# A two-layer graph and attention network on one core: softmax row sums folded by DMA, and three smaller edits

## The chip, the core and the metric

The kernel runs on one core of a Trainium2 chip. The core has a matrix engine (TensorE, PE in the profile), a vector engine (VectorE, DVE), a scalar engine (ScalarE, ACT), a general engine (GpSimd, POOL) and a queue engine that issues transfers (SyncE, SP). Each works through its own instructions in order[...]. The metric is device time in microseconds (us) of the whole program, lower is better. Everything is in 32-bit floats.

## The reference

The input x is 16 batches of 1024 nodes with 256 channels; adj is a 1024 x 1024 matrix. Cut to what matters:

```python
# layer 0
A_hat = A_norm * dinv[:, None] * dinv[None, :]
agg = jnp.einsum('nm,bmd->bnd', A_hat, features)
h = jax.nn.relu(_batchnorm(agg.reshape(-1, d) @ W1.T + b1, g1, be1))
out = _batchnorm(h @ W2.T + b2, g2, be2)
x = _layernorm(x + out)
# layer 1
c_adj = mean of x over channels                      # one number per node
Wg = adj * 2 * | |sigmoid(c_m - c_n) - 0.5| - 0.5 |  # gates, per batch
q = relu(einsum('bcn,bnm->bcm', x^T, Wg) * para)     # queries, 4 heads of 64
k, v = split(x @ kv_w)
attn = softmax(q k^T * scale)
x = _layernorm(x + attn @ v)
```

The batch norms need statistics over all batches, so layer 0 runs in two phases before layer 1 can begin.

## The kernel before

**Layer 0.** The first phase (to about 607 us) multiplies the normalised adjacency with x and then with W1 for every batch, and keeps statistics; products of 2 x 2 blocks are formed with seven multiplications (`seven`, L104). Results go to DRAM in units of half a batch (four chunks of 128 x 512), except the last four units, those of batches 14 and 15, which stay in SBUF. The second phase (L454 to L547, to about 800 us) normalises each chunk with a ReLU on ScalarE (`first`, L476), combines chunks on DVE and POOL (L488, L509 to L513), multiplies by W2 and by sums of blocks of W2 (`SV`, L463 to L467), and stores the result. It starts with the two batches that stayed, whose 16 chunks L525 to L528 normalise before anything else on ScalarE.

**Layer 1: `fast` (L571).** Batches follow one another. One batch of attention is 16 steps: two halves of 512 queries, times two pairs of heads, times four steps over the keys. A step is `scores` (q and k on PE into PSUM, L787), `exps` (ScalarE, L799, one step ahead), `sums` (DVE adds the exponentials into an accumulator `acc` of 128 partitions x 2 heads x 512 queries, L805 and L808) and `attend` (PE multiplies with v, L823). At the fourth step ScalarE and DVE form the output `ot` (L834, L835), which goes to DRAM (`put_o`). Four steps make a block; a batch has four blocks, one for each pair in each half. "Third block" below means first pair of the second half.

Between the blocks stand the pieces of other work: the next batch's gates (`wg_a` on ScalarE, `wg_b` on DVE), its keys and values (L736, L747, from `x1T`), its queries (`graph`, L761), and for the batch after that the loading (`load`), scaling (`bn2_q`, POOL, L614), transposing (`rows`, DVE, L618), layer norm (`ln1_a` with statistics on DVE and POOL, `ln1_b` on ScalarE, L646), and the way of the result through DRAM back into `x1T` (`put_x1`, `get_x1`, and `x1_v` on DVE, L669). `crow` (L683) broadcasts the channel means through DRAM; the gates read it.

**Row sums.** `acc` holds, for each query, 128 partial sums on 128 partitions. `dens` (L846) adds them up with four matmuls by a column of ones (L852), ScalarE copies the result (L854), and four small transfers put it beside `ot` in DRAM, in rows 256 and up of `o_dram` (`DR` = 8 rows for each head). `fetch_o` (L881) loads output and sums back with eight transfers for a half, `finish_a` (L891) transposes both in one DVE instruction (L900), takes reciprocals (L903), scales (L905), adds the residual (L910) and takes the statistics of the layer norm; `finish_b` (L919) applies it on ScalarE and stores. The last half of the last batch (`by_pe`, L812) skips DRAM: `back` (L874) transposes on PE, `recips` (L863) the sums.

**The order.** A table gives each piece a slot; a slot is two steps, a block is two slots. `put` (L961) enters a piece, `arrange` (L1052) orders the pieces of a slot by `rank` (L1033), and the loop at L1178 issues all pieces of a block's two slots, then its four steps. `between` holds pieces that are issued behind a given step instead. `sums` of a block's first step is issued behind the last "short" PE piece of the block (`behind`, L1181; `dens` is one), or at the very front when there is none. Each engine's queue follows this order.

```python
            for k in range(len(now) + 1):
                if k == behind and 0 <= g < nsteps:
                    sums(g)
                if k < len(now):
                    f, a = now[k]
                    f(*a)
```

Pools concerned: `accp` (2 accumulators, L405), `ob` (2 fetched tiles), `ps_t` (4 PSUM tiles for all but the scores), `ps_s` (2 PSUM tiles for the scores), `ep` (6 exponential tiles, three steps).

Of the kernel before, what the change touches and what calls it, by code (L numbers as in the profile page):

```python
# [9 lines left out]
F32 = mybir.dt.float32  # L10
AF = mybir.ActivationFunctionType
OP = mybir.AluOpType
AX = mybir.AxisListType
# [3 lines left out]
P = 128  # L17
EPS = 1e-5
HEADS = 4
# [3 lines left out]
def gnn_norm_attention_kernel(  # L23
# [57 lines left out]
    Q = 32  # L81
# [1 line left out]
    y_blk = [yT_all[b].rearrange("i (d e) (q n) -> q e (i d) n", e=Q, q=NQ) for b in range(B)]  # L83


    DR = 8
    CD = C + HEADS * DR
    o_dram = {(b, h): dram.tile([NT // NH, CD, P], F32, name=f"o{b}_{h}") for b in range(B) for h in range(NH)}
    x1_dram = {
# [39 lines left out]
    with ExitStack() as l0:  # L129
        w0 = l0.enter_context(tc.tile_pool(name="w0", bufs=1))  # L130
        hp = l0.enter_context(tc.tile_pool(name="hp", bufs=9))
        W1T = w0.tile([P, CT, H], F32, name="W1T")
        W2T = w0.tile([P, HT, C], F32, name="W2T")
# [4 lines left out]
        hT = {}  # L138
# [10 lines left out]
        def bn_affine(mv, rs, c, g, be, bias, s, t, name):  # L149
# [6 lines left out]
            nc.vector.tensor_mul(s[:, col], rs, g[:, col])  # L156
            nc.vector.scalar_tensor_tensor(t[:, col], mu, s[:, col], be[:, col], op0=OP.mult, op1=OP.add)

        s1 = w0.tile([P, HT], F32, name="s1")
        t1 = w0.tile([P, HT], F32, name="t1")  # L160

        with ExitStack() as ph1:
# [220 lines left out]
            for b in range(B):  # L383
                other = hidden_blocks(b - 1) if b > 0 else iter(())
                for k, _ in enumerate(aggregate(b)):
                    next(other, None)
                    if b > 0 and k == 3:
                        sums_x(b + 1)
                for _ in other:
                    pass  # L390
            for f in range(HT):
                for h in range(NH):
                    u = (B - 1) * NH + h
                    if f == 0:
                        hT[u] = hp.tile([P, HT, FB], F32, tag="h", name=f"hT{u}")
                    p = hidden(B - 1, h, f)
                    nc.scalar.copy(hT[u][:, f, :], p)
                    nc.vector.bn_stats(st1[:, f, u, :], p)
                bn_affine(*bn_moments(st1, f, "bn1"), f, g1t, be1t, b1t, s1, t1, "bn1")
# [2 lines left out]
        right = lambda name, bufs: ctx.enter_context(tc.tile_pool(name=name, bufs=bufs, side="right"))  # L402
        keep = right("keep", 1)
        ldp = right("ldp", LDP)
        accp = right("accp", 2)  # L405
        RD = keep.tile([P, B * NT + 1, HEADS], F32, name="RD")
        ones32 = keep.tile([P, 32], F32, name="ones32")
        stq = keep.tile([P, 2, C // Q], F32, name="stq")
# [45 lines left out]
        with ExitStack() as ph2:  # L454
# [3 lines left out]

            KF = HT // 2
            wq = [[W2T[:, j * KF : (j + 1) * KF, ts(i, P)] for j in range(2)] for i in range(CT)]
            SV = tmp.tile([P, 4, KF, P], F32, tag="SV", bufs=1, name="SV")  # L463
            nc.gpsimd.tensor_add(SV[:, 0], wq[1][0], wq[1][1])
            nc.gpsimd.tensor_sub(SV[:, 1], SV[:, 0], wq[0][0])
            nc.gpsimd.tensor_sub(SV[:, 2], wq[0][0], wq[1][0])
            nc.gpsimd.tensor_sub(SV[:, 3], wq[0][1], SV[:, 1])  # L467
            ws = {1: wq[0][0], 2: wq[0][1], 3: SV[:, 3], 4: wq[1][1], 5: SV[:, 0], 6: SV[:, 1], 7: SV[:, 2]}
            KB_ = KEEP // NH
            pairs = [list(range(B - KB_, B))] + [[b, b + 1] for b in range(0, B - KB_, 2)]  # L470
# [5 lines left out]
            def first(u, fs=range(HT)):  # L476
                for f in fs:
                    nc.scalar.activation(
                        hT[u][:, f, :], hT[u][:, f, :], AF.Relu, bias=t1[:, f : f + 1], scale=s1[:, f : f + 1]
                    )  # L480
# [41 lines left out]
                                hT.pop(u_)  # L522
                    yield

            for fs in (range(KF), range(KF, HT)):  # L525
                for h in range(NH):
                    for b in pairs[0]:
                        first(b * NH + h, fs)  # L528
            for k, pair in enumerate(pairs):
                ahead = [b * NH + h for b in pairs[k + 1] for h in range(NH)] if k + 1 < len(pairs) else []  # L530
                for u in ahead:
# [21 lines left out]
    NP = HEADS // 2  # L553
# [17 lines left out]
    def fast():  # L571
      with ExitStack() as fx:
# [202 lines left out]
        def step(g):  # L775
            b, s = divmod(g, NS)
            hf, pair, cp = s // (NP * NT // 2), s // (NT // 2) % NP, s % (NT // 2)
            return b, hf, pair, cp
# [17 lines left out]
        def exps(g):  # L796
            for a in range(2):
                E[g, a] = ep.tile([P, 2, FB], F32, tag="e", name=f"e{g}_{a}")
                nc.scalar.activation(E[g, a], S.pop((g, a)), AF.Exp)  # L799

        def sums(g):
            b, hf, pair, cp = step(g)
            if cp == 0:
                ACC[b, hf, pair] = accp.tile([P, 2, FB], F32, tag="acc", name=f"acc{g}")
                nc.vector.tensor_add(ACC[b, hf, pair], E[g, 0], E[g, 1])  # L805
            else:
                for a in range(2):
                    nc.vector.tensor_add(ACC[b, hf, pair], ACC[b, hf, pair], E[g, a])  # L808
# [2 lines left out]

        def by_pe(b, hf):  # L812
            return b == B - 1 and hf == NH - 1

        def attend(g):
            b, hf, pair, cp = step(g)
# [24 lines left out]
        def put_o(b, hf, rows_, t):  # L841
            nc.sync.dma_start(
                o_dram[b, hf][:, rows_, :].rearrange("i p n -> p i n"), t.rearrange("p (i n) -> p i n", n=P)
            )

        def dens(b, hf):  # L846
            p = ps_t.tile([P, FB], F32, tag="t", name="pd")
            for pair in range(NP):
                acc = ACC.pop((b, hf, pair))
                for h in range(2):  # L850
                    k = 32 * (2 * pair + h)
                    nc.tensor.matmul(p[k : k + 32, :], ones32, acc[:, h, :], start=True, stop=True)  # L852
            DT[b, hf] = otp.tile([P, FB], F32, tag="dt", bufs=1, name=f"dt{b}_{hf}")
            nc.scalar.copy(DT[b, hf], p)  # L854
            if not by_pe(b, hf):
                for k in range(HEADS):
                    put_o(b, hf, slice(C + k * DR, C + (k + 1) * DR), DT[b, hf][32 * k : 32 * k + DR, :])

# [32 lines left out]
        def finish_a(b, j):  # L891
            hf, k = divmod(2 * j, KB)
            pool_r = (rp, "r") if b < B - 1 or not by_pe(b, hf) else (x1p, "x1")
            rd = RD[:, b * NT + 2 * j : b * NT + 2 * j + 2, :]
            if by_pe(b, hf):
                r = pool_r[0].tile([P, 2, C], F32, tag=pool_r[1], name=f"r_{b}_{j}")
                p = OB.pop((b, j))
            else:
                t = pool_r[0].tile([P, 2, CD], F32, tag=pool_r[1], name=f"r_{b}_{j}")
                nc.vector.transpose(  # L900
                    t.rearrange("p a c -> p (a c)"), OB.pop((b, j)).rearrange("p a c -> p (a c)")
                )
                nc.vector.reciprocal(rd, t[:, :, C:].rearrange("p a (h r) -> p a h r", r=DR)[:, :, :, 0])  # L903
                p = r = t[:, :, :C]
            nc.vector.tensor_mul(  # L905
                r.rearrange("p a (h d) -> p a h d", h=HEADS),
                p.rearrange("p a (h d) -> p a h d", h=HEADS),
                rd.unsqueeze(3).to_broadcast([P, 2, HEADS, HD]),
            )
            nc.vector.tensor_add(r, r, x1s.pop((b, j)))  # L910
            mv, rs = ln_stats(sm, r, f"z{b}_{j}")
            nm = sm.tile([P, 2], F32, tag="nm", name=f"nm_{b}_{j}")
            for a in range(2):
                nc.gpsimd.tensor_scalar(
                    nm[:, a : a + 1], mv[:, a, 0:1], rs[:, a : a + 1], -1.0, op0=OP.mult, op1=OP.mult
                )
            R[b, j] = (r, rs, nm)
# [43 lines left out]
        def put(w, t, f, *a):  # L961
            at.setdefault(w * NC + t, []).append((f, a))
# [4 lines left out]
        for b in range(B):  # L967

            for hf in range(NH):
                t = (hf + 1) * (NC // NH)  # L970
                put(b, t, dens, b, hf)
                if by_pe(b, hf):
                    put(b, t, recips, b, hf)
                for k in range(KB // 2):
                    j = hf * (KB // 2) + k

                    if b * NH + hf < B * NH - 3:
                        t_f, t_a, t_b = (t + 1, t + 2 + k, t + 6 + k) if hf == 0 else (t + 1, t + 4 + k, t + 6 + k)
                    elif not by_pe(b, hf):

                        t_f, t_a, t_b = t, t + 2 * k, t + 2 + 2 * k if b < B - 1 else (t + 2, NC + 1)[k]
                        if b == B - 1 and k == 0:
                            between[(b * NC + t_b) * 2 + NK // 2] = [(finish_b, (b, j))]
                            t_b = None
                    else:
                        t_f, t_a, t_b = t, t + 1 + k, t + 2 + k
                    put(b, t_f, back if by_pe(b, hf) else fetch_o, b, j)
                    if t_a == t:
                        between[(b * NC + t) * 2 + NK // 2] = [(finish_a, (b, j))]
                    else:  # L990
                        put(b, t_a, finish_a, b, j)
                    if t_b is not None:
                        put(b, t_b, finish_b, b, j)
# [36 lines left out]
        nsteps = B * NS  # L1030


        order = (dens, recips, x1_t, finish_a, fetch_o, finish_b, x1_v, rows, ln1_a, ln1_b, put_x1, get_x1, means, load, crow)  # L1033
        rank = {f: k for k, f in enumerate(order)}
        short = (dens, recips, x1_t, back)

# [327 lines left out]
```

## Time and profile before

| | us |
|---|---|
| median of 10 runs (2459.5 to 2462.69) | 2460.13 |
| the profiled execution: its own time | 2459.8 |
| its span, first to last instruction | 2458.1 |
| attention stage, about | 880 to 2430 |

| group | count | mean ns |
|---|---|---|
| L808 DVE add into acc | 384 | 1325 |
| L799 ACT exponential | 512 | 1020 |
| L852 PE row-sum matmul instructions | 256 | 612 |
| L854 ACT copy of the row sums | 32 | 588 |
| L900 DVE transpose in `finish_a` | 62 | 768 |
| L669 DVE transpose into x1T | 56 | 699 |
| L478 ACT normalisation of a chunk of layer 0, kept units | 16 | 801 |

In a timeline line the first number is the start in us from the span's beginning, the second the time that the merged run of instructions took, then engine, source line, operation, output<-input, shapes and how often; a bracket gives the idle time before it and what ended it. Matmuls of several column groups overlap, so the busy time of a group (the first number behind the bar in a group's row) says more than its mean. A table of windows gives, for a stretch, the busy time of PE, PE's weight loads, DVE, ACT and POOL, then PE's granted clock, the share of the 16 DMA engines and GB/s. The program issues each 32-bit matmul as two PE instructions.

### The profile page before, as it was taken

The numbers are of one execution on the slowest core, as the hardware profiler recorded it, in microseconds if no ns is written. First come the engines' busy times: TensorE is split into PE (matmuls) and PEld (weight loads), VectorE is DVE, ScalarE is ACT, GpSimd is POOL, SyncE is SP. The second block draws the span as 40 slices with busy tenths as digits, with TensorE's granted clock in tenths as the row PEclk, the third lists the DMA queues.
The fourth block names the chain that finished last, engine by engine and source line by source line (L and its number), as shares of the span: only waits on it lengthen the run. The fifth ranks groups of instructions, "written<-read, shape, count | busy, mean of one in ns | idle before, by whom it ended". The sixth has DMA issues, their size and how long they took to land. (4 is left out here: it accounts for less than half of the span.)

```text
span 2458.1 us, 33873 instructions
## 1 busy us (share of the span) xinstructions
PE 2409.4 (98%) x12217; PEld 1007.1 (41%) x12217; DVE 1810.9 (74%) x2583; ACT 1093.9 (45%) x1549; POOL 776.0 (32%) x826
## 2 busy tenths in 40 slices
PE   8999999999999899999999999999999999999997
PEld 4444444444444443443434434344344343443432
DVE  5545545556776777888788888888888878888676
ACT  2000000002554455564655656656566465564644
POOL 2222232221556531414224133232342322414012
PEclk9999999999999999999999999999999999999998
DMA  3122122222578544544544535545364454554221
GB/s 137 69 86 103 69 86 103 88 83 86 202 271 275 133 121 87 139 126 111 144 106 124 147 87 150 119 120 149 82 149 110 121 146 97 138 129 108 68 43 51
DMA packets 583951, 292.73 MB, mean 119 GB/s; under 512 B 407528, under 2 KB 556512, under 8 KB 576608
## 3 DMA queue, kind: packets, MB, share of 16 engines
q1 hardware_dynamic: 583776, 290.49, 43.2%
q8 instruction: 98, 1.61, 0.3%
q14 instruction: 77, 0.63, 0.1%
HBM read 194.46 MB, written 95.94 MB: 118 GB/s over the span
## 5 line engine op out<-in xcount | busy, mean ns | idle before, releaser
L799 ACT ACTIVATE e<-s 128x1024 f32<-128x1024 f32 x512 | 495.8, 1020 | 327.7 <-PE s L787 264.7
L808 DVE TENSOR_TENSOR acc<-acc,e 128x1024 f32<-128x1024 f32 x384 | 508.7, 1325 | 112.8 <-ACT e L799 86.5
L787 PE MATMUL s<-qT,kT 64*64 64x512 f32 x4096 | 490.6, 594 | 4.4 <-ACT e L799 1.7
L823 PE MATMUL o<-e,v 64*64 64x512 f32 x4096 | 485.3, 589 | 0.0
L761 PE MATMUL pg<-wg,x 128*128 128x512 f32 x960 | 426.5, 597 | 0.0
L614 POOL TENSOR_TENSOR yt<-yt,stq 128x512 f32<-128x512 f32 x120 | 183.8, 1532 | 412.9 <-DMA yt<-yT 236.0
L761 PEld LDWEIGHTS pg<-wg,x 128*128 128x128 f32 x960 | 178.7, 190 | 238.6 <-issue 237.8
L823 PEld LDWEIGHTS o<-e,v 64*64 64x64 f32 x4096 | 156.6, 133 | 282.8 <-issue 275.1
L787 PEld LDWEIGHTS s<-qT,kT 64*64 64x64 f32 x4096 | 147.2, 133 | 298.4 <-issue 254.1
L107 ACT COPY u<-pa 128x512 f32<-128x512 f32 x15 | 8.8, 585 | 475.3 <-PE pa L312 475.3
L66 POOL TENSOR_SCALAR rs_z<-mv_z 128x2 f32<-128x2 f32 x64 | 18.2, 285 | 470.6 <-DVE mv_z L563 449.7
L720 DVE SCALAR_TENSOR_TENSOR wg<-wg,adj 128x1024 f32<-128x1024 f32 x128 | 163.5, 1308 | 2.8
L312 PE MATMUL pa<-AhT,x 128*128 128x512 f32 x360 | 161.8, 592 | 0.0
L646 ACT ACTIVATE x<-x,nm_a,rs_a 128x256 f32<-128x256 f32 x128 | 75.8, 594 | 171.6 <-POOL nm_a L636 171.2
L835 DVE TENSOR_TENSOR ot<-o,ot 128x512 f32<-128x512 f32 x64 | 44.3, 691 | 130.9 <-ACT ot L834 130.9
L747 PE MATMUL pv<-kvw,x1T 128*128 128x256 f32 x512 | 118.2, 384 | 0.0
L736 PE MATMUL pk<-x1T,kvw 128*128 128x512 f32 x256 | 117.9, 604 | 0.0
L343 PE MATMUL ph<-agg,SW 128*128 128x512 f32 x240 | 112.8, 592 | 0.0
L66 POOL TENSOR_SCALAR rs_a<-mv_a 128x2 f32<-128x2 f32 x64 | 38.0, 593 | 234.6 <-DVE mv_a L563 233.4
L747 PEld LDWEIGHTS pv<-kvw,x1T 128*128 128x128 f32 x512 | 96.8, 192 | 31.7 <-issue 16.2
L312 PE MATMUL pa<-T,sx 128*128 128x512 f32 x240 | 107.9, 592 | 0.0
L312 PEld LDWEIGHTS pa<-AhT,x 128*128 128x128 f32 x360 | 68.4, 190 | 86.1 <-issue 86.1
(193 smaller groups left out, 3142.3 us busy)
## 6 DMA issues: line engine op xcount, KB each, us to landing
adj<-in_adj_dram SPq DMA_DIRECT2D x128, 512.0 KB
h<-hT SPq DMA_DIRECT2D x28, 1024.0 KB
hL<-h SPq DMA_DIRECT2D x28, 1024.0 KB
ob<-o SPq DMA_DIRECT2D x248, 72.0 KB
x<-in_x_dram SPq DMA_DIRECT2D x16, 1024.0 KB
yT<-y SPq DMA_DIRECT2D x64, 256.0 KB
out_dram<-r SPq DMA_DIRECT2D x64, 256.0 KB
xr<-in_x_dram SPq DMA_DIRECT2D x62, 256.0 KB
```

The costliest lines, as they stand in the source:

```text
L312: nc.tensor.matmul(p, xs[n][:, k, :], bs[n][:, k, :], start=(k == 0), stop=(k == KN - 1))
L343: nc.tensor.matmul(p, ws[n][:, ts(f, P)], bs[n], start=True, stop=True)
L614: nc.gpsimd.tensor_tensor(y, y, sc, op)
L646: nc.scalar.activation(r, r, AF.Identity, bias=nm[:, a : a + 1], scale=rs[:, a : a + 1], accum_out=css[b][:, i : i + 1])
L720: nc.vector.scalar_tensor_tensor(t, t, 1.0, adjs[b * NT + i], op0=OP.add, op1=OP.mult)
L736: nc.tensor.matmul(p, kvw[:, k, ts(c, P)], x1Ts[b][:, k, ts(h, FB)], start=(k == 0), stop=(k == CT - 1))
L747: nc.tensor.matmul(p[:, ts(a, C)], x1Ts[b][:, k, ts(j + a, P)], kvw[:, k, C:], start=(k == 0), stop=(k == CT - 1),)
L761: nc.tensor.matmul(pg[b], x1s[b, k // 2][:, k % 2, ts(c, P)], wgs[b, k][:, ts(h, FB)], start=(k == 0), stop=(k == NT - 1))
L787: nc.tensor.matmul(t[r * HD : (r + 1) * HD, h, :], kTs[b, pair][h * HD : (h + 1) * HD, ts(2 * cb + r, HD)], qTs[b, pair, hf][h * HD : (h + ...
L799: nc.scalar.activation(E[g, a], S.pop((g, a)), AF.Exp)
L808: nc.vector.tensor_add(ACC[b, hf, pair], ACC[b, hf, pair], E[g, a])
L823: nc.tensor.matmul(O[b, hf, pair][r][h * HD : (h + 1) * HD, :], vs[b][r * HD : (r + 1) * HD, cb, pair * P + h * HD : pair * P + (h + 1) * HD],
```

## The change

Three things change in layer 1 and one in layer 0.

1. **Row sums through DMA.** For all but the last three halves (`by_dma`), `dens` is gone. Instead POOL issues two accumulating transfers for each pair (`fold`): partitions 64 to 127 of `acc` are added onto 0 to 63, then, behind the block's second step, 32 to 63 onto 0 to 31. A block later `put_den` writes the remaining 32 rows for each head to DRAM. So `DR` is 32 instead of 8, `fetch_o` loads 384 rows instead of 288 and comes two slots later, and `finish_a` transposes sums and output in two instructions and adds the 32 rows with a `tensor_reduce`. `accp` has three buffers. For the first half of a batch `finish_a` moves from the start of the fourth block to behind the block's second and fourth steps.
2. **Last step of the program.** Its exponentials aren't added into `acc` on DVE; the row-sum matmuls of the last pair take them as further operands.
3. **Last pair of output tiles** is scaled with eight ScalarE instructions instead of one on DVE.
4. **Second phase's first chunks.** The first unit of each of the two batches comes first on ScalarE; of the next unit two chunks are normalised on DVE (two instructions each); the block sums of W2 (`SV`) are formed before the first phase's end instead of behind it.

```diff
-    DR = 8
+    DR = Q
...
+            SV = w0.tile([P, 4, KF, P], F32, name="SV")
+            wq = [[W2T[:, j * KF : (j + 1) * KF, ts(i, P)] for j in range(2)] for i in range(CT)]
+            nc.gpsimd.tensor_add(SV[:, 0], wq[1][0], wq[1][1])
...
-        accp = right("accp", 2)
+        accp = right("accp", 3)
...
-            for fs in (range(KF), range(KF, HT)):
-                for h in range(NH):
-                    for b in pairs[0]:
-                        first(b * NH + h, fs)
+            for fs in (range(KF), (KF,), (KF + 1,)):
+                for b in pairs[0]:
+                    first(b * NH, fs)
+            u = pairs[0][0] * NH + 1
+            for f in range(KF, HT):
+                t = hT[u][:, f, :]
+                nc.vector.tensor_scalar(t, t, s1[:, f : f + 1], t1[:, f : f + 1], op0=OP.mult, op1=OP.add)
+                nc.vector.tensor_scalar(t, t, 0.0, None, op0=OP.max)
+            first(u, range(KF))
+            for b in pairs[0][1:]:
+                first(b * NH + 1)
...
         def sums(g):
             b, hf, pair, cp = step(g)
+            if g == nsteps - 1:
+
+                EX[b, hf, pair] = [E[g, a] for a in range(2)]
+                return
...
+        def by_dma(b, hf):
+            return b * NH + hf < B * NH - 3
+
+        def fold(b, hf, pair, n):
+            acc = ACC[b, hf, pair]
+            nc.gpsimd.dma_start(acc[:n], acc[n : 2 * n], accum_op=OP.add)
+
+        def put_den(b, hf, pair):
+            acc = ACC.pop((b, hf, pair))
+            for h in range(2):
+                r = C + (2 * pair + h) * DR
+                put_o(b, hf, slice(r, r + DR), acc[:DR, h, :])
...
-                    nc.tensor.matmul(p[k : k + 32, :], ones32, acc[:, h, :], start=True, stop=True)
+                    more = EX.get((b, hf, pair), [])
+                    for n, t in enumerate(more + [acc]):
+                        nc.tensor.matmul(
+                            p[k : k + 32, :], ones32, t[:, h, :], start=n == 0, stop=n == len(more)
+                        )
...
+                p = r = pool_r[0].tile([P, 2, C], F32, tag=pool_r[1], name=f"r_{b}_{j}")
+                den = otp.tile([P, 2, CD - C], F32, tag="den", bufs=1, name=f"den_{b}_{j}")
+                ob = OB.pop((b, j))
+                nc.vector.transpose(den, ob[:, :, C:])
+                nc.vector.transpose(r, ob[:, :, :C])
+                den = den.rearrange("p a (h r) -> p a h r", r=DR)
+                if by_dma(b, hf):
+                    nc.vector.tensor_reduce(rd, den, AX.X, OP.add)
+                    nc.vector.reciprocal(rd, rd)
+                else:
+                    nc.vector.reciprocal(rd, den[:, :, :, 0])
+            if j == NT // 2 - 1 and by_pe(b, hf):
+
+                for a in range(2):
+                    for h in range(HEADS):
+                        nc.scalar.mul(r[:, a, ts(h, HD)], p[:, a, ts(h, HD)], rd[:, a, h : h + 1])
...
-                put(b, t, dens, b, hf)
+                if by_dma(b, hf):
+                    for pair in range(NP):
+
+                        s = b * NC + t + 2 * (pair - NP + 1)
+                        put(0, s + 1, fold, b, hf, pair, P // 2)
+                        between.setdefault(2 * s + 1, []).append((fold, (b, hf, pair, P // 4)))
+                        put(0, s + 2, put_den, b, hf, pair)
+                else:
+                    put(b, t, dens, b, hf)
...
-                        t_f, t_a, t_b = (t + 1, t + 2 + k, t + 6 + k) if hf == 0 else (t + 1, t + 4 + k, t + 6 + k)
+                        t_f, t_a, t_b = (t + 3, None, t + 6 + k) if hf == 0 else (t + 3, t + 4 + k, t + 6 + k)
+                        if hf == 0:
+                            between.setdefault((b * NC + t + 2) * 2 + 2 * k + 1, []).append((finish_a, (b, j)))
```

More of the change, by code (lines that the diff above doesn't have):

```diff
@@ L157, in bn_affine @@
             nc.vector.scalar_tensor_tensor(t[:, col], mu, s[:, col], be[:, col], op0=OP.mult, op1=OP.add)
+        KF = HT // 2
         s1 = w0.tile([P, HT], F32, name="s1")
@@ L390, in gnn_norm_attention_kernel @@
                     pass
+            SV = w0.tile([P, 4, KF, P], F32, name="SV")
+            wq = [[W2T[:, j * KF : (j + 1) * KF, ts(i, P)] for j in range(2)] for i in range(CT)]
+            nc.gpsimd.tensor_add(SV[:, 0], wq[1][0], wq[1][1])
+            nc.gpsimd.tensor_sub(SV[:, 1], SV[:, 0], wq[0][0])
+            nc.gpsimd.tensor_sub(SV[:, 2], wq[0][0], wq[1][0])
+            nc.gpsimd.tensor_sub(SV[:, 3], wq[0][1], SV[:, 1])
             for f in range(HT):
@@ L457, in gnn_norm_attention_kernel @@
             ps = ph2.enter_context(tc.tile_pool(name="ps2", bufs=8, space=PSUM, reuse_waits="tile"))
[L461 to L467, printed above, removed]
             ws = {1: wq[0][0], 2: wq[0][1], 3: SV[:, 3], 4: wq[1][1], 5: SV[:, 0], 6: SV[:, 1], 7: SV[:, 2]}
@@ L799, in exps @@
                 nc.scalar.activation(E[g, a], S.pop((g, a)), AF.Exp)
+        EX = {}
         def sums(g):
             b, hf, pair, cp = step(g)
+            if g == nsteps - 1:
+                EX[b, hf, pair] = [E[g, a] for a in range(2)]
+                return
             if cp == 0:
@@ L898, in finish_a @@
             else:
-                t = pool_r[0].tile([P, 2, CD], F32, tag=pool_r[1], name=f"r_{b}_{j}")
-                nc.vector.transpose(
-                    t.rearrange("p a c -> p (a c)"), OB.pop((b, j)).rearrange("p a c -> p (a c)")
-                )
[L903 to L909, printed above, removed]
+                p = r = pool_r[0].tile([P, 2, C], F32, tag=pool_r[1], name=f"r_{b}_{j}")
[14 more added lines that the diff above has]
+            else:
+                nc.vector.tensor_mul(
+                    r.rearrange("p a (h d) -> p a h d", h=HEADS),
+                    p.rearrange("p a (h d) -> p a h d", h=HEADS),
+                    rd.unsqueeze(3).to_broadcast([P, 2, HEADS, HD]),
+                )
             nc.vector.tensor_add(r, r, x1s.pop((b, j)))
@@ L970, in fast @@
                 t = (hf + 1) * (NC // NH)
-                put(b, t, dens, b, hf)
+                if by_dma(b, hf):
[4 more added lines that the diff above has]
+                        put(0, s + 2, put_den, b, hf, pair)
+                else:
+                    put(b, t, dens, b, hf)
                 if by_pe(b, hf):
@@ L982, in fast @@
                         if b == B - 1 and k == 0:
-                            between[(b * NC + t_b) * 2 + NK // 2] = [(finish_b, (b, j))]
+                            between.setdefault((b * NC + t_b) * 2 + NK // 2, []).append((finish_b, (b, j)))
                             t_b = None
@@ L988, in fast @@
                     if t_a == t:
-                        between[(b * NC + t) * 2 + NK // 2] = [(finish_a, (b, j))]
-                    else:
+                        between.setdefault((b * NC + t) * 2 + NK // 2, []).append((finish_a, (b, j)))
+                    elif t_a is not None:
                         put(b, t_a, finish_a, b, j)
@@ L1030, in fast @@
         nsteps = B * NS
-        order = (dens, recips, x1_t, finish_a, fetch_o, finish_b, x1_v, rows, ln1_a, ln1_b, put_x1, get_x1, means, load, crow)
+        order = (dens, recips, x1_t, put_den, finish_a, fetch_o, finish_b, x1_v, rows, ln1_a, ln1_b, put_x1, get_x1, means, load, crow)
         rank = {f: k for k, f in enumerate(order)}
```

## The prediction

> **What bounds the kernel now.** I read four views. First the page's busy times and the table of windows, to see which engine fills the long attention stage (from about 880 us to 2430 us):
>
> ```profile
> PE 2409.4 (98%) x12217; PEld 1007.1 (41%) x12217; DVE 1810.9 (74%) x2583; ACT 1093.9 (45%) x1549; POOL 776.0 (32%) x826
> ...
> 1200.00:1400.00 200.00, 199.74 (x1279) 79.40 (x1278) 166.44 (x229) 116.89 (x164) 65.22 (x80) 1.00 0.50 123
> ```
>
> PE is busy 199.74 of 200 us there, DVE 166, so PE sets the stage: a matmul removed is a gain, and any wait put on PE is a loss. Second, PE's timeline around a row-sum matmul (L852), and that group's row:
>
> ```profile
> 1023.35 1.13 PE L761 MATMUL pg<-wg,x 128*128 128x512 f32 x2
> 1024.40 1.06 PE L852 MATMUL pd<-acc,ones 128*32 128x512 f32 x8
> 1025.40 7.99 PE L761 MATMUL pg<-wg,x 128*128 128x512 f32 x18
> ...
> L852 PE MATMUL pd<-acc,ones 128*32 128x512 f32 x256 | 36.0, 612 | 3.2 <-DVE acc L808 3.2
> ```
>
> 18 pg matmuls take 7.92 us to the next start, so 0.44 each; the two at 1023.35 would end at 1024.23. From there to 1025.40 one half's row sums cost 1.17 us of PE; the same sum at 1071.72 gives 1.19. I take 1.18.
>
> Third, where one batch ends and the next begins (1071.72), on PE and DVE. There the next batch's keys (L736) need the second half of x1T, which DVE transposes at L669:
>
> ```profile
> 1071.72 1.98 PE L736 MATMUL pk<-x1T,kvw 128*128 128x512 f32 x4
> 1073.63 1.07 PE L852 MATMUL pd<-acc,ones 128*32 128x512 f32 x8
> 1074.63 5.42 PE L736 MATMUL pk<-x1T,kvw 128*128 128x512 f32 x12
> ...
> 1055.32 0.76 DVE L900 STREAM_TRANSPOSE r<-ob 128x576 f32<-128x576 f32 x1
> 1058.97 0.71 DVE L669 STREAM_TRANSPOSE x1T<-xb 128x512 f32<-128x512 f32 x1
> 1072.44 0.69 DVE L835 TENSOR_TENSOR ot<-o,ot 128x512 f32<-128x512 f32 x1 [2.94 <-ACT ot L834]
> 1073.05 1.29 DVE L669 STREAM_TRANSPOSE x1T<-xb 128x512 f32<-128x512 f32 x2
> 1074.73 1.23 DVE L805 TENSOR_TENSOR acc<-e,e 128x1024 f32<-128x1024 f32 x1 [0.39 <-PE pd L852]
> ```
>
> The first two DVE lines bracket one whole `finish_a`: 3.63 us. The last three show that DVE does L669 right behind the output sum L835, done at 1074.34, before the third key matmul group (about 1076.35). Slack 2 us.
>
> Fourth, the third block of a batch, where ScalarE's normalisation (L646) stands ahead of the exponentials:
>
> ```profile
> 1033.94 0.60 ACT L646 ACTIVATE x<-x,nm_a,rs_a 128x256 f32<-128x256 f32 x1 [7.80 <-POOL nm_a L636]
> 1035.27 1.92 ACT L799 ACTIVATE e<-s 128x1024 f32<-128x1024 f32 x2
> 1036.81 1.90 PE L787 MATMUL s<-qT,kT 64*64 64x512 f32 x16
> ```
>
> PE's scores at 1036.81 reuse the PSUM tile that the exponential at 1035.27 frees about 0.97 us later: slack 0.5 us.
>
> [...] two row-sum adds (L808) take 3.21 us beside L614 at 1018.53, 2.55 alone at 1066.95; POOL's rs_a takes 1.02 us beside L805 at 1031.18, 0.22 elsewhere.
>
> **The change, part by part.**
>
> (1) Row sums off PE. `by_dma` holds for 29 of 32 halves: 29 x 1.18 = 34.2 us of PE gone, at once. The 29 ScalarE copies (L854, 588 ns) go too; ScalarE has room, so nothing.
>
> (2) What takes their place: per half four folds on POOL, four 64 KB writes on SP for four of 16 KB, eight fetches of 96 KB for eight of 72. POOL is a third busy. A second fold waits for the first one's landing, with POOL's queue behind it[...], covered because the next POOL work (L614, then rs_z) waits longer for data: before, 236 us for yT. Cost 0, at worst about 2.5 us a batch where it delays nm_a. The fetches run at 7.16 us for eight at 1029.13, so 9.5 us for a third more. They move one block later: into the block with get_x1 and crow, and into the block whose DMA share is already 0.93 to 0.99 at 1003 to 1013. SP's queue behind them holds xb, crow_d and crow. I put crow's issue at about 1068 instead of 1063.29; ScalarE first reads it at 1072.30. Hidden, but barely.
>
> (3) `finish_a` grows. Two transposes for one: 128x512 costs 0.70 (L669), 128x576 0.77, so 128x256 about 0.45: +0.40. The reduce of 128x256: rows of 644 ns for 480 and 1214 for 1024 elements give about 0.41. So 3.63 becomes 4.45 us. On DVE's total it is small (58 x 0.8 = 47 us on 166 of 200 busy); where it stands in the queue matters.
>
> (4) `finish_a` of the first half moves: from the start of the fourth block to behind its second and fourth step. DVE's new order at the batch's end is L835, finish_a, L805, then both L669 (L805 rises because no row-sum matmul stands ahead of it). The instruction order shows the third key group waiting for the second L669. From the traced times: L835 ends at 1073.05; + 4.45 = 1077.50; + 1.15 for L805 = 1078.65; + 1.34 = 1080.0. PE, without L852, wants it at 1071.72 + 2 x 1.72 = 1075.16. **PE waits 4.9 us.** The first moved finish_a doesn't delay L835: sums to 1062.5, finish_a to 1067.0, four adds to 1072.2, L835 at 1072.44. The wait falls at the ends of batches 0 to 13: 14 x 4.9 = 68.6 us. Bounds: 4.0 (finish_a at its old length) to 6.5 (a fetch that lands 2 us late); I take 4.9.
>
> (5) Third block. DVE: L835, then L805 (+1.15, earlier than before), finish_a (+0.8), then rows and statistics: mv_a 2.0 us later, 9.5 us after the block's start. POOL's rs_a to nm_a takes 1.4 (uncontended) to 2.8 (as traced, beside L805), then L646 twice 1.33, then the exponential 0.97: 13.4 to 14.7 us after the start. PE wants the tile at 8.79 + 1.77 + 1.72 = 12.3. Wait 1.1 to 2.4; I take 1.5, in 13 batches: 19.5 us.
>
> (6) Second phase's opening. ScalarE does 14 chunks instead of 16 (0.71 each), the four 0.44 us DVE operations and two of ScalarE's complete one unit at about 615.1 instead of 617.97, and SV leaves DVE's way (L156 and L157 took 0.74 and 0.76 us beside it, 0.16 and 0.22 else). PE idles 8.2 us there now:
>
> ```profile
> 607.97 11.38 ACT L478 ACTIVATE hT<-hT,t,s 128x512 f32<-128x512 f32 x16
> 614.47 3.70 PE L494 MATMUL po<-hT,W2T 128*128 128x512 f32 x8 [1.94 <-ACT hT L478]
> 620.67 1.96 PE L494 MATMUL po<-hT,SV 128*128 128x512 f32 x4 [2.50 <-DVE hT L509]
> 625.01 5.42 PE L494 MATMUL po<-hT,SV 128*128 128x512 f32 x12 [2.38 <-DVE hT L509]
> ```
>
> Gain 1 to 4, taken 2.5; PE is full from there to 800, so it is kept.
>
> (7) The end. DVE leads it from 2420.68, after 2.01 us of waiting for ob:
>
> ```profile
> 2420.68 0.78 DVE L900 STREAM_TRANSPOSE r<-ob 128x576 f32<-128x576 f32 x1 [2.01 <-DMA ob<-o]
> 2432.17 7.86 DVE L808 TENSOR_TENSOR acc<-acc,e 128x1024 f32<-128x1024 f32 x6
> 2440.09 1.92 PE L852 MATMUL pd<-acc,ones 128*32 128x512 f32 x4 [3.16 <-DVE acc L808]
> ```
>
> Two adds go (-2.6); two finish_a grow by 0.4 (+0.8); the larger ob lands later (+0.6); the matmuls after the last add run one column group after another, about 2.8 us for 1.92 (+0.9); the last DVE scaling (0.66) goes beside ScalarE's (-0.7). Sum -1.0, between -3 and +1.
>
> **Sum.** Against the profiled execution's own 2459.8 us (span 2458.1; the median of ten runs is 2460.13, so the two are the same): -34.2 - 2.5 - 1.0 + 68.6 + 19.5 = +50.4, so **2510 us**. Own range: stalls of 4.0 and 1.1 give 2490, of 6.5 and 2.4 give 2545.
>
> **Rivals.**
> (B) The waits don't appear and PE keeps the gain: 2459.8 - 37.7 = 2422. For it: PE is full and DVE has 17% idle. Against: the order on DVE and the wait of the third key group are in the program. It wins if L669 ends by 1075.2; the turning point is 34.2 + 3.5 = 37.7 us of waits, 2.7 us a batch over 14.
> (C) Transfers add to it: folds, writes and fetches form a chain on POOL and SP, and ob or crow arrives late in the fourth block. 2.5 us more a batch: 2510 + 35 = 2545. For it: DMA shares near 1 at 1003 to 1013 and SP's full queue; against: ob is wanted only at 1062.
> (D) The waits are about half of mine (2.7 us a batch) and cancel the gain: 2460.
>
> **How the numbers follow.** Forecast 0.68, B 0.15, C 0.12, D 0.05. A measurement of this kernel can tell 0.2% (4.9 us) from no change. Faster: B and a little of D, 0.16; within: 0.04 of D; slower: 0.80. The range 2450 to 2560 leaves out B and a little above C.
>
> **What would show it.** In the trace of after: PE's third L736 group at a batch's start waiting some 5 us for DVE x1T; PE L787 in the third block waiting for ACT e by 1 to 2.5 us; row-sum matmuls left for the last three halves alone; PE's share in the attention stage falling from 99.9% to about 94%. Wrong if PE stays at 99% there, or if PE's waits name DMA-fed tiles (ob, crow) instead.

## The result, and the profile after

| | before | after |
|---|---|---|
| median, us | 2459.98 (28 runs, 2458.43 to 2462.72) | 2543.43 (8 runs, 2539.74 to 2547.8) |
| span of the profiled execution, us | 2458.1 | 2542.1 |

The ratio is 1.0337, 95% interval 1.0328 to 1.0346. The forecast was 2510 us, range 2450 to 2560.

The page's busy times, and then the table of windows for the same 200 us as before (columns: busy us of PE, PE's weight loads, DVE, ACT and POOL with instructions, then PE's clock, DMA share, GB/s):

```profile
PE 2411.1 (95%) x11993; PEld 1010.8 (40%) x11993; DVE 1850.7 (73%) x2704; ACT 1080.2 (42%) x1526; POOL 895.7 (35%) x942
```

```profile
1200.00:1400.00 200.00, 189.20 (x1202) 75.83 (x1194) 162.24 (x237) 109.74 (x153) 75.67 (x91) 0.99 0.65 136
```

PE was busy 199.74 of these 200 us; now it is 189.20. There are 224 matmul instructions fewer in the program, yet PE's busy total rose from 2409.4 to 2411.1 us. So there are two losses: PE waits, and some of its matmuls take longer. The view of waits for PE says for what it waits (us in total, times, longest):

```profile
PE pk L746 <- DVE x1T L679: 60.7, 14, 4.3
PE s L797 <- ACT e L809: 23.4, 14, 4.6
```

Both lines are new in this form: before, PE waited for x1T not at all, and once for an exponential. PE's timeline and then DVE's show one of the 14 batch starts:

```profile
1074.82 3.70 PE L746 MATMUL pk<-x1T,kvw 128*128 128x512 f32 x8
1082.85 5.36 PE L746 MATMUL pk<-x1T,kvw 128*128 128x512 f32 x8 [4.33 <-DVE x1T L679]
1088.05 1.89 PE L757 MATMUL pv<-kvw,x1T 128*128 128x256 f32 x8
```

```profile
1075.54 0.69 DVE L867 TENSOR_TENSOR ot<-o,ot 128x512 f32<-128x512 f32 x1 [0.58 <-ACT ot L866]
1076.14 0.43 DVE L938 STREAM_TRANSPOSE den<-ob 128x256 f32<-128x256 f32 x1
...
1080.28 1.21 DVE L821 TENSOR_TENSOR acc<-e,e 128x1024 f32<-128x1024 f32 x1
1081.41 1.30 DVE L679 STREAM_TRANSPOSE x1T<-xb 128x512 f32<-128x512 f32 x2
```

DVE runs without a gap: output sum, `finish_a` (1076.14 to 1080.28), first row-sum add, both transposes. PE resumes at 1082.85. The second eight matmul instructions are the same work as the first eight, which took 3.70 us; they took 5.36. The page's row of this group has both losses, busy time and mean to the left, the wait to the right:

```profile
L746 PE MATMUL pk<-x1T,kvw 128*128 128x512 f32 x256 | 143.2, 712 | 60.7 <-DVE x1T L679 60.7
```

Before, the row had 117.9 us and a mean of 604 ns. 143.2 - 117.9 = 25.3 us are slower matmuls.

To see where 84.0 us of span went, I take the time from one block's output copy on ScalarE (L834, in the changed kernel L866) to the next block's, as the timelines give it, and add up the differences:

```
part                                          before    after    difference, us
attention's first copy (opening gain in it)   895.08    893.78     -1.3
row sums off PE: 29 halves x 1.19                                  -34.5
14 batch starts, without row sums             23.10     29.51 mean +89.7
13 third blocks, without row sums             22.67     24.40 mean +22.5
last batch's first two blocks                 30.58     35.86      +5.3
last batch's third copy to ScalarE's last work 29.08    26.52      -2.6
from there to the end of the span              5.03     10.18      +5.15
sum                                                                +84.2
```

The last row isn't in the prediction. The instructions at the program's last line tell what it is (before, then after; columns: minimum/median/maximum duration in ns, first and last start):

```profile
L1359 POOLq DRAIN  x3: 34/50/82, 2452.8 to 2457.8; - x3
```

```profile
L1416 POOLq DRAIN  x3: 34/98/9538, 2531.8 to 2541.9; - x3
```

POOL's queue ends the program with a drain that took 0.05 us and now takes 9.54 us, from 2531.8 to 2541.3. SyncE is through at 2536.7, so some 5 us of it stand bare at the end.

### The profile page after: what moved, and what is told of

Same layout as the page of the kernel before. It is cut to its first block, busy times and chain, and to the rows that moved or that the text cites. A ratio compares the mean times of both kernels' runs of the same rounds, so it can differ in the third digit from the quotient of the medians.

```text
span 2542.1 us, 33754 instructions
## 1 busy us (share of the span) xinstructions
PE 2411.1 (95%) x11993; PEld 1010.8 (40%) x11993; DVE 1850.7 (73%) x2704; ACT 1080.2 (42%) x1526; POOL 895.7 (35%) x942
## 5 line engine op out<-in xcount | busy, mean ns | idle before, releaser
L809 ACT ACTIVATE e<-s 128x1024 f32<-128x1024 f32 x512 | 495.8, 1019 | 324.3 <-PE s L797 286.9
L797 PE MATMUL s<-qT,kT 64*64 64x512 f32 x4096 | 493.6, 597 | 26.1 <-ACT e L809 23.4
L66 POOL TENSOR_SCALAR rs_z<-mv_z 128x2 f32<-128x2 f32 x64 | 41.5, 648 | 480.4 <-DVE mv_z L573 371.8
L746 PE MATMUL pk<-x1T,kvw 128*128 128x512 f32 x256 | 143.2, 712 | 60.7 <-DVE x1T L679 60.7
L839 POOL DMA_DIRECT2D acc<-acc x116 | 97.8, 845 | 215.6 <-DMA acc<-acc 183.9
L656 ACT ACTIVATE x<-x,nm_a,rs_a 128x256 f32<-128x256 f32 x128 | 75.7, 593 | 198.4 <-DVE RD L943 127.3
L66 POOL TENSOR_SCALAR rs_a<-mv_a 128x2 f32<-128x2 f32 x64 | 26.8, 419 | 248.6 <-DVE mv_a L573 234.0
L746 PEld LDWEIGHTS pk<-x1T,kvw 128*128 128x128 f32 x256 | 55.7, 228 | 146.2 <-issue 145.9
```

The costliest lines, as they stand in the source:

```text
L746: nc.tensor.matmul(p, kvw[:, k, ts(c, P)], x1Ts[b][:, k, ts(h, FB)], start=(k == 0), stop=(k == CT - 1))
L797: nc.tensor.matmul(t[r * HD : (r + 1) * HD, h, :], kTs[b, pair][h * HD : (h + 1) * HD, ts(2 * cb + r, HD)], qTs[b, pair, hf][h * HD : (h + ...
L839: nc.gpsimd.dma_start(acc[:n], acc[n : 2 * n], accum_op=OP.add)
```

## The experiments

Theory "order": VectorE's new order makes PE wait, and the idle makes the matmuls behind it slow. Rival "transfers" (case C of the prediction, taken as the main cause): folds, row-sum writes and larger fetches on POOL's and SP's queues hold the kernel back. For the rival spoke that the DMA share had risen from 0.50 to 0.65 in the window above.

**1. One `finish_a` elsewhere.** The second `finish_a` of a batch's first half goes from behind the last step of its batch to behind the first step of the next.

```diff
-    between.setdefault((b * NC + t + 2) * 2 + 2 * k + 1, []).append((finish_a, (b, j)))
+    between.setdefault((b * NC + t + 2) * 2 + 3 * k + 1, []).append((finish_a, (b, j)))
```

> The changed kernel with one finish_a in another place: the second one of a batch's first half stands behind the first step of the next batch (behind the key transposes) instead of behind the last step of its own. Theory 'order' (VectorE's order makes TensorE wait for x1T, 4.3 us of idle and then 1.75 us of slower key matmuls, 14 times): 2543 - 14 x 6.1 = 2458, with up to 10 us to either side for what finish_a then delays in the next batch. Rival 'transfers' (folds, row-sum writes and fetches on GpSimd and SyncE's queues hold the kernel back): 2535 to 2545, no change, since not one transfer moves.

Measured: 2466.59 us, ratio to the kernel before 1.0028 (1.002 to 1.0037). One DVE group in another place, 14 times, gives back 77 us; all transfers are as they were. (The 14 starts gave back all but 0.45 us each; the third blocks became 6 us longer in sum, 28.7 for 22.5; two of them make up most of this, at 26.9 us, where PE's waits of 2.23 and 2.52 us were followed by slow matmuls.) PE's timeline at the same batch start:

```profile
1069.99 3.70 PE L746 MATMUL pk<-x1T,kvw 128*128 128x512 f32 x8
1073.90 3.67 PE L746 MATMUL pk<-x1T,kvw 128*128 128x512 f32 x8 [0.20 <-DVE x1T L679]
```

The wait is 0.20 us, and the second group again takes as long as the first. "Transfers" is out as the main cause.

**2. The first add behind the transposes.** Only the first row-sum add of a batch moves.

```diff
-    behind = max((k + 1 for k, fa in enumerate(now) if is_short(fa)), default=0)
+    behind = max((k + 1 for k, fa in enumerate(now) if is_short(fa) or fa[0] is x1_v), default=0)
```

> The changed kernel with the first row-sum add of a batch (1.2 us) put behind the two transposes into x1T instead of ahead of them. Theory 'order': TensorE's wait falls from 4.3 to about 3.1 us at 14 batch starts, 2543 - 14 x 1.2 = 2526. [...] Rival 'transfers': 2540 to 2545.

Measured: 2521.91 us, ratio 1.0244 (1.0229 to 1.026), 4 us below the figure of "order"; had all slow matmuls gone with the wait, it would be 2543 - 14 x (1.2 + 1.75) = 2502. The wait fell to 3.30 us at all 14 starts, as expected, but the slow stretch went at only six of them. PE's timeline at two starts of the same run:

```profile
977.56 3.67 PE L746 MATMUL pk<-x1T,kvw 128*128 128x512 f32 x8 [3.30 <-DVE x1T L679]
...
1081.20 5.37 PE L746 MATMUL pk<-x1T,kvw 128*128 128x512 f32 x8 [3.30 <-DVE x1T L679]
```

Same wait, same work, 3.67 and 5.37 us. So the slow stretch isn't a property of the work, and whether it comes isn't settled by the length of the idle alone.

The trace also records the clock that TensorE was granted. Here are two stretches of 3.41 us at each of these starts (first number behind the length: PE's busy us; third from the end: the granted clock):

```profile
972.68:976.09 3.41, 1.58 (x4) 0.38 (x2) 3.20 (x9) 2.92 (x5) 0.00 (x0) 1.00 0.73 135
976.09:979.50 3.41, 1.94 (x5) 1.02 (x6) 3.38 (x6) 0.87 (x1) 3.03 (x4) 1.00 0.37 62
1078.49:1081.90 3.41, 0.70 (x2) 0.49 (x3) 3.31 (x8) 2.12 (x3) 1.49 (x3) 1.00 0.29 55
1081.90:1085.31 3.41, 3.41 (x5) 1.35 (x4) 3.34 (x5) 1.00 (x2) 2.19 (x2) 0.50 0.45 73
```

At the first start the wait is split, 1.83 and 1.47 us of idle in the two stretches, and the clock stays full. At the second 2.71 us of it lie in one stretch, and the next one runs at half the clock. At all eight slow starts the trace has such a half-clock stretch, at the six others none. Why stretches of 3.41 us, experiments 10 and 11 show.

**3. The ends alone.** Row sums of all halves on PE again, no fold, fetch and `finish_a` where they were; what stays of the change is the opening of the second phase and the end.

```diff
 def by_dma(b, hf):
-    return b * NH + hf < B * NH - 3
+    return False
...
-    t_f, t_a, t_b = (t + 3, None, t + 6 + k) if hf == 0 else (t + 3, t + 4 + k, t + 6 + k)
-    if hf == 0:
-        between.setdefault((b * NC + t + 2) * 2 + 2 * k + 1, []).append((finish_a, (b, j)))
+    t_f, t_a, t_b = (t + 1, t + 2 + k, t + 6 + k) if hf == 0 else (t + 1, t + 4 + k, t + 6 + k)
```

> The changed kernel with row sums of all halves back on TensorE, no fold, and fetch and finish_a where they were before: what is left is the opening of the second phase, the last step's weights straight into the row sums, and the last pair's scaling on ScalarE. By the traces the opening gave 2.35 us, and the computing at the end is 2.6 us shorter behind the last step's start: 2460 - 5 = 2455. Rival (the span of the changed kernel behind its last row-sum block, 24.8 us against 22.2, is the end's own cost): 2460 - 2.4 + 2.6 = 2460.

Measured: 2457.24 us, ratio 0.9988 (0.9981 to 0.9994): a gain, smaller than expected by 2 us. In its trace the opening gains 2.35 us and the last block 3.4; against that the first phase ends 1.06 us later, and the last batch's second block is 1.07 us longer, because the longer `finish_a` lets PE wait 2.74 us there instead of 1.68. From ScalarE's last work to the end it takes 5.0 us: without folds, no long drain.

**4. One DMA from GpSimd.** The kernel before, with one small fold in the first phase.

```diff
+        dm = w0.tile([P, Q], F32, name="dm")
+        nc.vector.memset(dm, 0.0)
+        nc.gpsimd.dma_start(dm[: P // 2], dm[P // 2 :], accum_op=OP.add)
```

> The kernel before with one small accumulating DMA issued by GpSimd in the first phase, its result unused. Theory: a kernel that has issued any DMA from GpSimd ends with a drain of GpSimd of 9.5 us (0.05 us before), of which the other engines' last work covers about 5: 2460 + 4.6 = 2464.6. Rival (the drain grows with the number of such DMAs, 174 in the changed kernel, or has another cause): 2460 to 2461.

Measured: 2461.21 us, ratio 1.0003 (0.9995 to 1.0011): no change, the theory of a fixed drain is wrong. The drain in its trace:

```profile
L1362 POOLq DRAIN  x3: 34/93/139, 2454.9 to 2460.6; - x3
```

0.14 us. (The expectation's count for the changed kernel is wrong: it issues 116 such DMAs, not 174.) Whether the number or the lateness of the DMAs counts was left for experiment 8.

**5. The third block.** Experiment 1's kernel; ScalarE's normalisation of x1's third piece goes behind the first step's exponentials.

```diff
+    if j == 2:
+        between.setdefault(((b - 2) * NC + 4) * 2, []).extend([(ln1_b, (b, j)), (put_x1, (b, j))])
+    else:
         put(b - 2, j + 3, ln1_b, b, j)
         put(b - 2, j + 3, put_x1, b, j)
```

> The first experiment's kernel, and in the third block of a batch ScalarE's normalisation of one piece of x1, with its write, goes behind the first step's exponentials instead of ahead of them. Theory: TensorE's waits there (13 blocks that are 28.7 us longer in all than the undisturbed ones) come only from the exponential standing behind that normalisation on ScalarE: 2466.6 - 28.7 = 2438. Rival: the exponentials are late for another reason (GpSimd, slowed by its folds, or the row sums on VectorE that free the weights' buffers): 2455 to 2467.

Measured: 2438.98 us, ratio 0.9912 (0.9895 to 0.9928); every third block is back at 22.67 us. ScalarE's timeline in the changed kernel and then here (L656 is the normalisation, L809 the exponential):

```profile
1037.57 0.60 ACT L656 ACTIVATE x<-x,nm_a,rs_a 128x256 f32<-128x256 f32 x1 [9.76 <-DVE RD L943]
...
1038.75 1.91 ACT L809 ACTIVATE e<-s 128x1024 f32<-128x1024 f32 x2
```

```profile
1128.87 1.94 ACT L809 ACTIVATE e<-s 128x1024 f32<-128x1024 f32 x2 [8.07 <-PE s L797]
1130.69 0.60 ACT L656 ACTIVATE x<-x,nm_a,rs_a 128x256 f32<-128x256 f32 x1
```

In the changed kernel the scores for that exponential were finished by 1036.67 (PE's timeline), while ScalarE still stood idle in front of the normalisation at the head of its queue:

```profile
1034.72 1.95 PE L797 MATMUL s<-qT,kT 64*64 64x512 f32 x16
```

With the edit the exponential waits for nothing but the scores.

**6. All orders mended.** Experiments 2 and 5 together, and in the last batch ScalarE's finish of the half before comes two slots later (`t + 4 + 2 * k` for `t + 2 + 2 * k`).

> The kernel of the third block's edit, with the first add of a batch behind the two transposes into x1T, and in the last batch ScalarE's finish of the half before two blocks' slots later. Theory: the 0.45 us that each of 14 batch starts still loses (6 us) and the second block of the last batch (4.35 us longer than before) go: 2438 - 10.5 = 2427. Rival: those two losses come from the folds or the fetches: 2435 to 2438. Either way this would be faster than both given kernels.

Measured: 2427.32 us, ratio 0.9862 (0.9846 to 0.9878): faster than both given kernels, and 5 us from the prediction's case B (2422). The window from 1200 to 1400 us:

```profile
1200.00:1400.00 200.00, 199.74 (x1260) 81.75 (x1259) 173.90 (x254) 115.91 (x160) 82.53 (x98) 1.00 0.72 153
```

PE is full again, with a DMA share of 0.72, higher than in the changed kernel's 0.65: the transfers were not in PE's way.

**7. All orders mended, row sums on PE.** Experiment 6's kernel, in which `by_dma` returns False.

> The kernel with all orders mended, but the row sums of every half back on TensorE and no fold. Theory: the row sums' matmuls cost 29 x 1.18 = 34.2 us on TensorE, and the folds cost nothing but the drain at the end (about 5 us): 2427 + 34 - 5 = 2456. Rival 'transfers': the folds cost more on the path than that, and this kernel is less than 20 us slower than the one with folds.

Measured: 2455.83 us, ratio 0.9981 (0.9972 to 0.9991): 28.5 us more than experiment 6. Here lies the worth of part (1) by itself: 29 x 1.19 = 34.5 us, less the bare 5 us of the drain, and 1 us that I did not follow further.

**8. Half of the folds.** `by_dma` holds for the first 16 halves.

> The kernel with all orders mended, folds for the first 16 halves alone (64 accumulating DMAs instead of 116, the last one some 750 us before the end), the others' row sums on TensorE. 13 x 1.18 = 15.3 us more on TensorE. If GpSimd's drain at the end grows with the number of its DMAs, it is 9.54 x 64 / 116 = 5.3 us, nearly all covered: 2427 + 15.3 - 4.5 = 2438. If it has one length wherever many such DMAs ran, it stays 9.5 us: 2442. If only late ones count, it is below 0.2 us, and the time 2437.

Measured: 2437.86 us, ratio 0.9905 (0.9888 to 0.9921). The drain:

```profile
L1419 POOLq DRAIN  x3: 34/98/5292, 2430.1 to 2436.0; - x3
```

1, 64 and 116 DMAs from GpSimd gave 0.14, 5.29 and 9.54 us, some 82 ns for each, and in this run the last of them was issued 750 us before the end. So the amount counts and the lateness doesn't. Whether it is their number or their bytes isn't shown: 64 and 116 have the same mix of sizes. About 5 us are covered by what the other engines do last.

**9. The last batch.** The two finishes go behind the second and the fourth step of the second block.

```diff
-    t_f, t_a, t_b = t, t + 2 * k, t + 4 + 2 * k if b < B - 1 else (t + 2, NC + 1)[k]
+    t_f, t_a, t_b = t, t + 2 * k, None if b < B - 1 else (t + 2, NC + 1)[k]
+    if b < B - 1:
+        between.setdefault((b * NC + t + 2) * 2 + 2 * k + 1, []).append((finish_b, (b, j)))
```

> The kernel with all orders mended, and the two finishes of the half before go, in the last batch, behind the second and the fourth step of its second block instead of ahead of its third and fourth. Theory: its third block (17.0 us, undisturbed 14.9) gets back the 2.1 us that these finishes cost there: 2427.3 - 2.1 = 2425.2. Rival: that block is longer for the row-sum matmuls that wait for the adds on VectorE (1.1 us), which this edit does not touch: 2426 to 2427.5.

Measured: 2427.25 us against experiment 6's 2427.32 (ratio to the kernel before 0.9866, 0.9849 to 0.9882). The four runs lie 3 us apart, so the medians alone can't settle an effect of 2 us; the trace does. The rival held: the third block took 17.02 us in experiment 6 and takes 17.01 here. PE's timeline in experiment 6 shows what makes it long:

```profile
2375.17 1.05 PE L886 MATMUL pd<-acc,ones 128*32 128x512 f32 x4
2377.31 1.05 PE L886 MATMUL pd<-acc,ones 128*32 128x512 f32 x4 [1.09 <-DVE acc L824]
```

The row sums of the second pair wait 1.09 us for DVE; and both pairs side by side take 1.06 us (x8), one after the other 1.05 each.

**10 and 11. The wait by itself.** Experiment 6's kernel; DVE repeats the last transpose into x1T, six times in all and then twelve.

```diff
-    nc.vector.transpose(x1Ts[b][:, :, ts(j, 2 * P)], XB.pop((b, j)).rearrange("p (c n) -> p c n", c=CT))
+    t = XB.pop((b, j)).rearrange("p (c n) -> p c n", c=CT)
+    for _ in range(6 if j == NT // 2 - 1 else 1):
+        nc.vector.transpose(x1Ts[b][:, :, ts(j, 2 * P)], t)
```

> The kernel with all orders mended, and the second transpose into x1T done six times over (same data, 0.65 us each), so that TensorE's third group of key matmuls waits about 5 x 0.65 - 1.0 = 2.2 us at each of 14 batch starts. Theory: an idle of 2.2 us is followed by matmuls at full rate, so each costs itself alone: 2427.3 + 14 x 2.2 = 2458. Rival: any wait there is followed by the 1.75 us of half-rate matmuls: 2427.3 + 14 x 3.95 = 2483.

> As the run with six transposes, but with twelve: an idle of about 11 x 0.65 - 1.0 = 6.2 us. Theory: 14 of 14 waits are followed by half-rate matmuls, 1.75 us each as behind 4.3 us: 2427.3 + 14 x 7.9 = 2538. Rival: the half-rate stretch grows with the idle, here to 2.5 us or more: 2549 or above.

Measured: 2493.89 us (ratio 1.014, 1.0123 to 1.0157) and 2564.48 us (ratio 1.0427, 1.041 to 1.0445). Both waits came out longer than I had sized them, 2.8 and 7.28 us. With six transposes the profile names ScalarE's gate as what ended 11 of the 14 waits, so the delay went by another queue too; only the idle's length is used here. One wait of each run:

```profile
1076.57 5.10 PE L748 MATMUL pk<-x1T,kvw 128*128 128x512 f32 x8 [2.96 <-DVE x1T L681]
```

```profile
1088.58 6.57 PE L748 MATMUL pk<-x1T,kvw 128*128 128x512 f32 x8 [7.28 <-DVE x1T L681]
```

After 2.8 us I had expected full rate: wrong, 13 of 14 are slow. After 7.28 us the slow stretch costs 2.3 us on average, more than behind 4.3 (1.8) and less than the rival's 2.5. Over all traces, PE waits of over 1 us in attention's key and score matmuls:

```
idle before, us   waits   slow behind   extra us where the key matmuls are slow
1.0 to 2.3          40         2
2.5 to 2.75          2         1
2.8 to 3.1          14        13        1.9
3.30                14         8        2.1
4.3 to 4.6          18        18        1.8
7.28                14        14        2.3
```

The two cases of the first row (waits of 1.88 us in experiment 2 and 2.23 us in experiment 1) show in the score matmuls and those with v behind the wait. In a slow stretch 3 to 7 starts of key matmul instructions lie some 853 ns apart where the others lie 429 ns apart: half the rate.

The record of the granted clock gives the rule behind this table. The half-clock stretches that end before their trace does last 3.413 us or two to four times that, and in each trace all of them begin on one grid of 3.413 us, to within 5 ns. I cut the attention stages of all 13 traces into the windows of this grid:

```
window     PE idle in it     next window at half clock
full clock 2.03 us or more   55 of 55
full clock 0.3 to 2.01 us     1 of 98 (1.88 us)
half clock 0.64 us or more   33 of 33
half clock 0.62 us or less    0 of 56
```

So it counts how much idle falls into one window, and where a wait lies on the grid decides. Of experiment 2's 14 equal waits the eight with half-rate matmuls behind them put 2.06 to 2.71 us into one window, the six others at most 1.98; the one wait of experiment 10 with full rate behind it is split into 1.22 and 1.58. The rule is read from attention alone: in layer 0 some windows don't follow it (four traces have one at about 813 us with 0.23 to 0.42 us of idle that was followed by another at half clock).

## Why the prediction was right, and where it was off

The sign, the place and the mechanism were right: PE loses row sums, and VectorE's order puts larger waits on it. The size was too small, +50.4 us for +84.0. By its steps:

- **(1)** -34.2 predicted; 29 x 1.19 = -34.5 by the blocks of experiments 6 and 7.
- **(2)** Cost 0 for the transfers. Right: experiment 1 moved no transfer and gave back 77 us, and experiment 6 fills PE with them. The folds land 4.3 and 3.2 us after their issue (medians), and POOL does block behind the second fold (4.2 us on average, 183.9 us in 44 waits); both are covered. What the step left out is the drain at the end, 9.54 us, 5 of them bare.
- **(3)** `finish_a` 4.45 us; 4.14 in the timeline above.
- **(4)** The term that was mis-sized. 14 x 4.9 = 68.6 us predicted, 89.7 measured. The idle was even a little shorter, 14 x 4.34 = 60.7 us, and came where and behind what was said. But the step priced a wait as its idle alone, and behind it the next matmuls run at half rate: 25.3 us more. (The trace has 54.6 us at half clock at the 14 starts, one window at twelve and two at the others. Idle and slow matmuls make 86.0 us; the other 3.7, some 0.3 us a wait, weren't followed.) A lone example stood in the profile of before: at its end 3.16 us of idle, and then four row-sum matmul instructions in 1.92 us that take 1.05 elsewhere; from 2439.24 us on its trace, too, records half the clock. The prediction quoted the line and didn't ask why.
- **(5)** 13 x 1.5 = 19.5 predicted, 22.5 measured, for the reason given, as experiment 5 shows. The idle alone is 23.4 - 4.6 = 18.8 us, or 1.45 a block. (The step's terms add up to 13.2 and 14.6 us, not to the 13.4 and 14.7 that it gives, so its waits should have read 0.9 to 2.3.)
- **(6)** -2.5 predicted, -2.35 from the second phase's start. The first phase ended 1.06 us later, so 1.3 remain. Both are in part luck with the clock. From ScalarE's first chunk to the end of the hundredth `po` instruction this opening takes 49.1 us, but 50.8 in six of the ten experiments that have it, a gain of only 0.65; in those six the trace has a half-clock window at 623 to 625 us, in the others none. (The opening of before takes 51.5, and 53.1 in experiment 4, which has such windows at 616 and 627 us.) And ScalarE's first chunk comes at 607.9 to 608.2 us in the traces without a half-clock window at 20 to 26 us, that of before among them, at 608.6 to 609.7 with one, as in the changed kernel, and at 610.0 with two.
- **(7)** -1.0 predicted. The computing is 2.6 us shorter, the drain makes the whole 2.6 us longer.
- **The last batch** (+5.3) was in no step. There is no next batch to wait, but the moved `finish_a` pushes the following ones on DVE; ScalarE's finish of a half stands ahead of an exponential and waits for them. ScalarE's timeline, then PE's:

```profile
2474.71 2.08 ACT L969 ACTIVATE r<-r,nm,rs_z 128x256 f32<-128x256 f32 x4 [3.37 <-POOL nm L961]
2476.69 1.91 ACT L809 ACTIVATE e<-s 128x1024 f32<-128x1024 f32 x2
```

```profile
2477.74 3.69 PE L797 MATMUL s<-qT,kT 64*64 64x512 f32 x16 [4.58 <-ACT e L809]
```

Case C's time (2545) was nearer than the forecast's, for a wrong reason: its 2.5 us a batch are about the slow matmuls and the last batch, not transfers.

What stays open: the 0.3 us that a wait costs beyond its idle and the slow matmuls, why windows of layer 0 depart from the rule, and whether number or bytes make the drain long.

## What to carry to other kernels

A wait on a full TensorE isn't priced by its idle alone: here one of 1.0 to 2.3 us cost itself in 38 of 40 cases, one of 2.8 us or more mostly cost 1.8 to 2.3 us on top, on average. So look at the granted clock behind a wait, not only at the wait. Taking work off the engine that bounds the kernel is half of the job; the other half is the order in which the engines that feed it get through their queues: the same four edits made the kernel 83 us slower in one order and 33 us faster in another, with three groups and one add moved by a few places. Before blaming transfers, move one instruction group and leave the transfers alone.

## What the runs showed of the hardware

- TensorE's half-clock stretches began on a grid of 3.413 us, fixed within a trace to 5 ns. In attention a full-clock window with 2.03 us of idle or more was followed by one at half clock in 55 of 55 cases, one with 0.3 to 2.01 us in 1 of 98.
- A drain on GpSimd at the program's end was the longer the more DMAs GpSimd had issued: 0.14 us for one, 5.29 for 64, 9.54 for 116.
- A fold of 256 KB landed 4.3 us after its issue, one of 128 KB 3.2 us (medians), and issuing one took POOL 845 ns on average. The view of DMAs of the changed kernel (KB each, median us from issue to landing), then the page's row of the group:

```profile
acc<-acc POOLq DMA_DIRECT2D x58, 256.0 KB, 4.3
acc<-acc POOLq DMA_DIRECT2D x58, 128.0 KB, 3.2
```

```profile
L839 POOL DMA_DIRECT2D acc<-acc x116 | 97.8, 845 | 215.6 <-DMA acc<-acc 183.9
```
